# One lane for a group's loads, partial sums spread over the gate products, and layer 1's rows kept on chip in a two-layer graph network

## The chip, the cores and the metric

The kernel runs on one core of one Trainium2 chip. The metric is the device time of one execution in microseconds (us). The program writes its instructions engine by engine: TensorE (PE in the profile, with PEld for its weight loads) multiplies matrices, VectorE (DVE), ScalarE (ACT) and GpSimd (POOL) work on elements, and DMAs are issued from the queues of SyncE (SP), ScalarE and GpSimd. Each engine takes its instructions in the order in which they were written down, so an instruction that waits holds up all that stand behind it on the same engine.

## The reference, cut to what matters

There are 128 graphs of 128 nodes with 256 features, all in f32. Layer 0 normalizes the rows, runs two convolutions along the nodes and a sum over neighbours, and mixes the results with a gated unit. Layer 1 runs five small graph convolutions over the first 25 nodes of each graph.

```python
h = relu(layernorm(x))                       # layer 0
x_conv = relu(bn2(conv17(relu(bn1(conv1(h))))) + h)
A = exp(-dist(h @ w_se.T)) * adj
x_nmp = A @ relu(h @ w_msg.T + b_msg)        # sum over neighbours
gi = concat(x_conv, x_nmp) @ w_ih.T + b_ih
gh = h @ w_hh.T + b_hh
r, z = sigmoid(gi_r + gh_r), sigmoid(gi_z + gh_z)
n = tanh(gi_n + r * gh_n)
x = x + (1 - z) * n + z * h
h = relu(layernorm(x))                       # layer 1, nodes 0 to 24
for g, nodes in enumerate(GROUPS):           # two graph convolutions each
    fused[nodes] += softmax(fusion_w)[g] * gcn(gcn(h[nodes], W1[g]), W2[g])
x = x + fused
```

## The kernel before

Four graphs make a group; there are 32 groups (q = 0 to 31). Sixteen graphs, that is four groups, make a block of layer 1; there are eight blocks. The kernel is written as Python generators. A generator writes some instructions and then yields two numbers: how much TensorE time they are thought to take, and how long its next step should be left alone. Generators stand in lanes, lanes have weights, and a small planner (`Order.run`) always takes a step from the ready lane that has had least for its weight. The order in which the steps are taken is the order of the instructions on every engine. No time of the chip enters into it.

The work falls into these stages:

- **Setup** (`fold`, `load_taps`): x of the first groups, the constants, the 1x1 weights `c1w` and the 17-tap weights come in. `fold` normalizes the first group.
- **Stage a** (`stage_a`, 16 groups at a time): moments of the rows (L272 to L275), normalization (L280), transpose (L390), ReLU to `hT` (L392), the 1x1 convolution (L401, bias added by VectorE in L404) and a Fourier transform over the nodes (L412). `tap_weights` runs beside it: products of the taps (L455), copied by ScalarE (L460) and VectorE (L462), written to DRAM.
- **Stage b** (`stage_b`, L502): the 17-tap convolution as products in the Fourier domain, once for each half of the groups. `early` runs beside all of this and computes the sums over neighbours (L571 to L618) ahead, which go to DRAM.
- **Group stage**: for each group, `stage_n` loads `hT` and the neighbour sums `xm` and makes the four differences `tm` of `xm` on VectorE (`sums`, L551 to L554). `stage_c` transforms the convolution back (L663), forms the gate products (L698, seven for r and z with `wrz`, seven half ones with `wn`, on 256 columns each in a fast scheme that needs the differences `th`, `tm` and `tc` of its three operands), L762 for the hidden part, and adds the products up on VectorE (L730 to L793). Then come tanh (L795), the mixing on GpSimd (L798 to L801), a transpose back (L814) and the addition of x (L817 to L820). The first 32 rows of each graph, which layer 1 needs, go to DRAM (`x1d`, L826), the other rows to the output (L827). `th` of the next group is made in one go after the last hidden product. Two of the programs `stage_n`, `stage_c` are in work at a time, in one lane.
- **Layer 1**: `prepare` builds the normalized adjacency of a block, and `rows_of_x` in its course loads the block's rows from DRAM (L907), takes the moments of all four groups at once, raises to the power -1/2 on GpSimd (L275), normalizes (L280) and clips at zero on GpSimd (L901). `block` multiplies (L986, L1003, L1012), turns and gathers (L1033, L1045, L1054) and adds the result to the rows. This lane has weight 0.36 against 1 of the groups. The last block takes its rows from the chip (`direct`).

The gate products are held in three PSUM banks (`pgat`): TensorE can be three products ahead of VectorE, and then waits for a bank. All other products share five banks (`ptmp`).

Of the kernel before, what the change touches and what calls it, by code (L numbers as in the profile page):

```python
# [9 lines left out]
FP = mybir.dt.float32  # L10
# [197 lines left out]
def kernel(ctx: ExitStack, tc: tile.TileContext, x, adj, consts, vecs, w_se, conv1_w,  # L208
# [17 lines left out]
    x1d = [dr.tile([SB, WIDE, D], FP, name=f"x1d{b}") for b in range(NBLK)]  # L226
# [144 lines left out]
    def stage_a(q):  # L371
        ab = LATE["ab"]
        for n in range(q, min(q + 2, (q // BQ + 1) * BQ)):
            if n not in XA:
                load_xa(n)
                if n == q:
                    yield 0.0, 6.0
# [19 lines left out]
        for h in range(2):  # L397
# [9 lines left out]
            yield 1.75, 2.0 * h  # L407
# [31 lines left out]
    def tap_weights():  # L439

        yield 0.0, 0.0
        for n in range(4):
            if n:
                if n < 3:
                    load_taps(n + 1, nc.sync, nc.gpsimd)
                if n == 1:
                    load_late()
            for m in range(8):
# [87 lines left out]
    EN, IN, IN2, X1, E_DONE = {}, {}, {}, {}, set()  # L536
# [8 lines left out]
    TH, HT, TM = {}, {}, {}  # L545

    def sums(name, q, x, bufs=1):


        t = LATE["co"].tile([P, 4, D], FP, tag=name, name=f"{name}{q}", bufs=bufs)  # L550
        nc.vector.tensor_sub(t[:, 0], x[:, 0, D:], x[:, 0, :D])  # L551
        nc.vector.tensor_sub(t[:, 1], x[:, 1, D:], t[:, 0])  # L552
        nc.vector.tensor_sub(t[:, 2], x[:, 1, D:], x[:, 0, D:])
        nc.vector.tensor_sub(t[:, 3], t[:, 1], x[:, 1, :D])  # L554
        return t
# [81 lines left out]
    def stage_n(q):  # L637
        hT = LATE["co"].tile([P, 2, 512], FP, tag="hT", name=f"hTc{q}", bufs=2)
# [4 lines left out]
        HT[q] = hT  # L643
        TM[q] = sums("tm", q, xm, bufs=2)
        IN[q] = hT, xm

    def stage_c(q):
        while not (q - 1 in G_DONE and q in IN):
            yield 0.0, 0.5
        (hT, xm), tm = IN.pop(q), TM.pop(q)  # L650
# [6 lines left out]
        th = TH.pop(q) if q in TH else sums("th", q, hT)  # L657
# [77 lines left out]
        tcs = sums("tc", q, xc)  # L735
# [7 lines left out]
        sigmoid(r2, r2, 0)  # L743
        yield 2.6, 0.0
# [6 lines left out]
        sigmoid(z2, z2, 2)  # L751
        yield 2.6, 0.0
# [3 lines left out]
        sigmoid(z1, z1, 2)  # L756
        yield 2.6, 0.0

        for dc in range(2):
# [6 lines left out]
            if dc and q + 1 in HT:  # L766
                TH[q + 1] = sums("th", q + 1, HT.pop(q + 1))
# [40 lines left out]
        direct = X1.get(q // QS)  # L808
        for h in range(2):
# [6 lines left out]
            if h == 0 and direct is not None:  # L816
                nc.vector.tensor_add(direct[:, q % QS], xt[:, 0], po[:, 0])  # L817
                nc.vector.tensor_add(xt[:, 1], xt[:, 1], po[:, 1])
            else:
                nc.vector.tensor_add(xt[:, 2 * h:2 * h + 2], xt[:, 2 * h:2 * h + 2], po)  # L820
        yield 0.9, 1.5
        for j in range(GB):
            rows = xt[j * WIDE:(j + 1) * WIDE]
            g = q * GB + j
            if direct is None:
                nc.gpsimd.dma_start(out=x1d[g // SB][g % SB], in_=rows[:, 0])  # L826
            nc.gpsimd.dma_start(out=out[g, WIDE:].rearrange("(t n) c -> n t c", n=WIDE),  # L827
                                in_=rows[:, 1:4])
# [3 lines left out]
    S, B1_DONE, P_DONE, Y_DONE = {}, set(), set(), set()  # L832

    def setup_1():
# [39 lines left out]
        last = NBLK - 1  # L874
        X1[last] = S["pool2"].tile([P, QS, D], FP, tag="x1l", name=f"x1_{last}", bufs=1)
        P_DONE.add(-1)
        B1_DONE.add(-1)
        Y_DONE.add(-1)
# [8 lines left out]
    def rows_of_x(blk, wait=True):  # L887

        ready = all(q in C_DONE for q in range(blk * QS, (blk + 1) * QS))
        if blk in S or not (wait or ready and blk - 1 in Y_DONE):  # L890
            return
        while not (all(q in C_DONE for q in range(blk * QS, (blk + 1) * QS))
                   and blk - 1 in Y_DONE):
            yield 0.0, 0.5
        if blk not in X1:
            load_x1(blk)
            yield 0.0, 6.0
        pool2 = S["pool2"]
        x1h = S[blk] = pool2.tile([P, QS, D], FP, tag="x1h", name=f"x1h{blk}", bufs=1)
# [239 lines left out]
```

## Time and profile before

| what | us | from |
|---|---|---|
| device time, median of 3 runs (2208.85 to 2214.99) | 2210.95 | the times |
| span of the profiled run | 2210.7 | the page |
| TensorE busy | 2079.8 (94%) | the page, part 1 |
| VectorE busy | 1198.4 (54%) | the page, part 1 |
| GpSimd busy | 788.4 (36%) | the page, part 1 |
| ScalarE busy | 690.1 (31%) | the page, part 1 |
| mean granted clock of TensorE | 0.971 | the times |
| last matmul ends at | 2196.6 | the timeline |

TensorE is busy for nearly the whole span, and the chain that ended last lies on it for 83%. The share of the other engines is an average over stages. The page's slices are 55 us long, so that a pause of 5 us is a tenth of one slice and hardly shows; pauses have to be looked for in the table of stretches of 50 us and in the timeline. "Idle before" in a timeline is the time that the engine did nothing before the instruction, with the instruction that ended it.

### The profile page before, as it was taken

To read this page: it belongs to the slowest core of one execution; us is meant where nothing else is said; L and a number is where in the kernel's file an instruction comes from. 1 tells how busy PE (TensorE), PEld (TensorE's weight loads), DVE (VectorE), ACT (ScalarE), POOL (GpSimd) and SP (SyncE) were. 2 spreads that over 40 slices of the span, in tenths; PEclk is the share of its full clock that TensorE was granted. 3 is DMA by queue.
4 is the path that set the end of the run, shared out by engine and by line. 5 is a ranking of instruction groups with operands and counts; after the bars stand their busy time and mean duration, and the time that the engine had idled before them with its cause. 6 is when DMAs were issued, how large, how long until landed. Compare 5 with 4: busy or idle time off the path is not lost.

```text
span 2210.7 us, 30635 instructions
## 1 busy us (share of the span) xinstructions
PE 2079.8 (94%) x11124; PEld 1636.9 (74%) x11124; DVE 1198.4 (54%) x2659; ACT 690.1 (31%) x1511; POOL 788.4 (36%) x990
## 2 busy tenths in 40 slices
PE   4999999899999999999999999999999999999967
PEld 2667888788888777777767778677777777776855
DVE  3765444676444547654554564564564565465541
ACT  2654222344322333223322322322322322322322
POOL 2431466231465234333332342252242333333140
PEclk8999999999999999999999999999999999999988
DMA  9986777744777734323232333232332322332211
GB/s 163 267 244 195 237 262 259 215 144 134 238 261 253 229 92 121 84 71 89 76 103 79 91 90 88 65 94 84 86 91 69 94 75 80 101 85 71 77 34 39
DMA packets 194359, 288.97 MB, mean 131 GB/s; under 512 B 22877, under 2 KB 145762, under 8 KB 194210
## 3 DMA queue, kind: packets, MB, share of 16 engines
q1 hardware_dynamic: 159794, 188.48, 30.0%
q0 software_dynamic: 33584, 97.81, 14.0%
q8 instruction: 88, 1.44, 0.3%
q10 hardware_dynamic: 832, 0.74, 0.2%
q14 instruction: 61, 0.50, 0.1%
HBM read 191.01 MB, written 95.94 MB: 130 GB/s over the span
## 4 chain that ended last, share of the span: by engine, by line
PE 83%; DVE 7%; DMA 4%; issue 2%; POOL 2%; ACT 1%; SPq 1%; DVEq 0%; ACTq 0%; POOLq 0%
PE p L698 33%; PE pa L502 6%; PE pg L762 5%; PE ph L1003 5%; PE pz L1012 5%; PE pm L591 4%; PE pc L401 4%; PE pb L502 3%; PE pi L663 3%; PE px L616 2%; PE pf L412 2%; DMA xa<-in_x 2%; PE pg L1045 1%; PE pc L677 1%; DVE st L272 1%
## 5 line engine op out<-in xcount | busy, mean ns | idle before, releaser
L798 POOL TENSOR_TENSOR d<-hTc,r 128x512 f32<-128x512 f32 x64 | 84.3, 1317 | 508.4 <-ACT r L795 495.7
L502 PE MATMUL pa<-wf,X 128*128 128x256 f32 x640 | 154.2, 385 | 0.0
L698 PE MATMUL p<-tc,wrz 128*128 128x256 f32 x512 | 133.0, 382 | 1.5 <-DVE tc L552 1.0
L698 PE MATMUL p<-th,wrz 128*128 128x256 f32 x512 | 134.2, 385 | 0.0
L698 PE MATMUL p<-tm,wrz 128*128 128x256 f32 x512 | 133.2, 383 | 0.0
L502 PEld LDWEIGHTS pa<-wf,X 128*128 128x128 f32 x640 | 119.3, 192 | 17.5 <-issue 2.8
L275 POOL TENSOR_TENSOR rs<-rs,cst 128x4 f32<-128x4 f32 x40 | 42.0, 1049 | 250.7 <-DVE rs L274 243.6
L525 DVE SCALAR_TENSOR_TENSOR y<-pa,kk 128x512 f32<-128x512 f32 x78 | 53.8, 690 | 142.7 <-ACT kk L524 142.5
L401 PE MATMUL pc<-c1w,hTa 128*128 128x256 f32 x512 | 127.6, 399 | 0.3 <-ACT hTa L392 0.3
L591 PE MATMUL pm<-wmsg,hT 128*128 128x256 f32 x512 | 121.2, 381 | 0.0
L401 PEld LDWEIGHTS pc<-c1w,hTa 128*128 128x128 f32 x512 | 98.3, 199 | 29.2 <-issue 6.4
L711 ACT ACTIVATE r<-r,brz 128x256 f32<-128x256 f32 x128 | 58.0, 500 | 186.5 <-DVE r L742 157.3
L762 PE MATMUL pg<-hTc,whn 128*128 128x512 f32 x256 | 116.0, 593 | 0.0
L826 POOL DMA_DIRECT2D x1d<-xt x112 | 59.3, 530 | 150.5 <-DVE xt L820 147.2
L698 PEld LDWEIGHTS p<-tc,wrz 128*128 128x128 f32 x512 | 97.5, 192 | 17.9 <-DVE tc L552 4.7
L1003 PE MATMUL ph<-yz,w 128*128 128x96 f32 (+3 forms) x640 | 108.3, 322 | 0.5 <-DVE yz L988 0.5
L698 PEld LDWEIGHTS p<-tm,wrz 128*128 128x128 f32 x512 | 98.5, 192 | 13.7
L1012 PE MATMUL pz<-hh,w 128*128 128x96 f32 (+3 forms) x640 | 107.4, 321 | 0.0
L698 PEld LDWEIGHTS p<-th,wrz 128*128 128x128 f32 x512 | 94.8, 190 | 16.9 <-issue 4.9
L591 PEld LDWEIGHTS pm<-wmsg,hT 128*128 128x128 f32 x512 | 95.9, 190 | 15.3 <-issue 2.1
L698 PE MATMUL p<-tm,wn 128*128 128x256 f32 x256 | 80.6, 397 | 24.2 <-DVE v L777 24.2
L1003 PEld LDWEIGHTS ph<-yz,w 128*128 128x128 f32 x640 | 87.1, 190 | 21.8 <-issue 15.8
(198 smaller groups left out, 4587.4 us busy)
## 6 DMA issues: line engine op xcount, KB each, us to landing
wf<-wfd SPq DMA_DIRECT2D x160, 256.0 KB, 4.0
wfd<-ws POOLq DMA_DIRECT2D x64, 320.0 KB, 6.2
yd<-y POOLq DMA_DIRECT2D x80, 256.0 KB, 3.8
yt<-yd SPq DMA_DIRECT2D x64, 320.0 KB, 4.1
w<-in_W SPq DMA_DIRECT2D x40, 512.0 KB, 4.0
xa<-in_x SPq DMA_DIRECT2D x128, 128.0 KB, 4.7
hTd<-hTa POOLq DMA_DIRECT2D x32, 512.0 KB, 4.8
hT<-hTd SPq DMA_DIRECT2D x32, 512.0 KB, 6.5
```

What stands on the lines that cost most here:

```text
L401: nc.tensor.matmul(pc[:, i], hT[:, k, (2 * h + i) * N:(2 * h + i + 1) * N], c1w[:, k], start=(k == 0), stop=(k == 1))
L502: nc.tensor.matmul(ps, xk(k), WF[f][:, k, s], start=(k == 0), stop=(k == 1))
L525: nc.vector.scalar_tensor_tensor(y, pa, 2.0, kk[:, None].to_broadcast([P, 2, D]), op0=ALU.mult, op1=ALU.subtract)
L591: nc.tensor.matmul(pm[:, i], hT[:, k, j * N:(j + 1) * N], wmsg[:, k], start=(k == 0), stop=(k == 1))
L663: nc.tensor.matmul(pi[b * 64:(b + 1) * 64], inv[:F], yt[:, b::2], start=True, stop=True)
L698: nc.tensor.matmul(ps[:, m], w[:, i, k, m * P:(m + 1) * P], factor(i, x, t), start=first and j == 0, stop=last and j == len(n) - 1)
L711: nc.scalar.activation(dst[:, m], src[:, m], AF.Sigmoid, bias=brz[:, b + m:b + m + 1])
L762: nc.tensor.matmul(pg, whn[:, k, dc * P:(dc + 1) * P], hT[:, k], start=(k == 0), stop=(k == 1))
L798: nc.gpsimd.tensor_sub(d, hT[:, dc], r[:, dc])
L826: nc.gpsimd.dma_start(out=x1d[g // SB][g % SB], in_=rows[:, 0])
L1003: nc.tensor.matmul(ph, w1[:, k, m * P:(m + 1) * P], yz[:, k, :, o:o + n], start=(k == 0), stop=(k == 1))
L1012: nc.tensor.matmul(pz, w2[:, g, m, cc * P:(cc + 1) * P], hs[g][:, m], start=(m == 0), stop=(m == 3))
```

## The change

The change has four parts.

1. **Start and stage a.** `c1w` and x of the second group come ahead of the taps, x of the third is asked for before `fold`, the second set of taps comes only in the course of the first one's products, and the tap products begin 16 units later. In the second half, groups after the first wait 14 units for their load where it was 6, and one pause of stage a is 2.8 where it was 2.
2. **A lane for the loads.** `stage_n` only loads `hT` and `xm` now, in a lane of its own, as soon as the group two before has finished its gates; `hT` has three buffers.
3. **Sums in pieces.** The eight differences of `hT` and `xm` of the next group are written two, two, two, one and one at a time, after the r and z products and the hidden products (`some_sums`). `th` has two buffers.
4. **Layer 1's rows on chip.** The transpose back writes its first rows into a tile of the block, of which there are three. The DRAM tensor, its 112 writes and 28 reads are gone. A lane `rows` takes the moments, the power, the normalization and the ReLU one group at a time; the ReLU is on ScalarE now. Layer 1 may start on a group as soon as its own rows are there. Its weight is 0.2 instead of 0.36.

No matrix product is added or taken away.

```diff
@@ stage_a, tap_weights
-                    yield 0.0, 6.0
+                    yield 0.0, 14.0 if q > BQ else 6.0
...
-            yield 1.75, 2.0 * h
+            yield 1.75, 2.8 * h
...
-        yield 0.0, 0.0
+        yield 0.0, 16.0
@@ sums
+    def some_sums(q, n):
+        if q in IN:
+            if q not in SUMS:
+                hT, xm = IN[q]
+                (th, a), (tm, b) = sums("th", q, hT), sums("tm", q, xm)
+                SUMS[q] = th, tm, a + b
+            while SUMS[q][2] and n != 0:
+                SUMS[q][2].pop(0)()
+                n = n and n - 1
@@ stage_n
-        hT = LATE["co"].tile([P, 2, 512], FP, tag="hT", name=f"hTc{q}", bufs=2)
+        while q > 1 and q - 2 not in G_DONE:
+            yield 0.0, 0.5
+        hT = LATE["co"].tile([P, 2, 512], FP, tag="hT", name=f"hTc{q}", bufs=3)
...
-        TM[q] = sums("tm", q, xm, bufs=2)
@@ stage_c
+        some_sums(q + 1, 2)
...
-            if dc and q + 1 in HT:
-                TH[q + 1] = sums("th", q + 1, HT.pop(q + 1))
+            some_sums(q + 1, 1)
...
+            X1[blk] = fr.tile([P, QS, D], FP, tag="x1", name=f"x1_{blk}", bufs=3)
...
-            if direct is None:
-                nc.gpsimd.dma_start(out=x1d[g // SB][g % SB], in_=rows[:, 0])
@@ rows, in place of rows_of_x
+        nc.vector.bn_stats(st, x1)
+        nc.vector.bn_aggr(mv, st)
+        nc.vector.tensor_scalar(rs, mv[:, 1:2], EPS, None, op0=ALU.add)
+        nc.gpsimd.tensor_tensor(rs, rs, c("mhalf")[:, :1], ALU.pow)
+        yield 0.0, 2.5
+        x1h = S["x1h", q] = S["pool"].tile([P, D], FP, tag="x1h", name=f"x1h{q}", bufs=5)
+        nc.vector.tensor_scalar(x1h, x1, mv[:, 0:1], rs, op0=ALU.subtract, op1=ALU.mult)
+        nc.scalar.activation(x1h, x1h, AF.Relu)
@@ start and lanes
-    load_taps(0, nc.sync, nc.gpsimd, nc.scalar)
     nc.scalar.dma_start(out=c1w, in_=conv1_w.rearrange("(k p) o -> p k o", p=P))
     load_xa(1)
+    load_taps(0, nc.sync, nc.gpsimd, nc.scalar)
+    load_xa(2)
     fold()
-    load_taps(1, nc.sync, nc.gpsimd)
...
-    groups = Lane([stage(q) for q in range(NQ) for stage in (stage_n, stage_c)], ahead=2)
+    loads = Lane([stage_n(q) for q in range(NQ)])
+    groups = Lane([stage_c(q) for q in range(NQ)], ahead=2)
...
-    order.run(groups, beside, Lane(second, ahead=2, weight=0.36))
+    order.run(loads, groups, beside, Lane([rows(q) for q in range(NQ)], ahead=2),
+              Lane(second, ahead=2, weight=0.2))
```

## The prediction

> **What bounds the kernel now.** First the page's parts 1 and 2: TensorE is busy 94% of the span, so only its pauses (2210.7 - 2079.8 = 131 us) and its slow clock can be gained; no product is removed. The clock row falls at both ends.
>
> ```profile
> PE 2079.8 (94%) x11124; PEld 1636.9 (74%) x11124; DVE 1198.4 (54%) x2659; ACT 690.1 (31%) x1511; POOL 788.4 (36%) x990
> ...
> PEclk8999999999999999999999999999999999999988
> ```
>
> Next I went through TensorE's timeline for pauses over 0.5 us. Apart from the first 15.6 us, in which nothing has arrived, four places hold most: 15.1 us from 23 to 38, 8.3 us from 406 to 414, seven pauses of 4.6 to 4.9 us between 936 and 1995, about 175 us apart (one for each layer-1 block but the last), and 16.7 us in three pieces from 2136 to 2155. The rest is about 30 us around stage a and 14 us for the last output after the last matmul.
>
> The start, from the timeline. DVE stands in front of the second group's x at 22.2 and of the third's at 35.2. Behind that wait is the copy of the tap products at 37.5, and TensorE, out of banks, waits for this copy.
>
> ```profile
> 35.18 0.43 DVE L272 BATCH_NORM_STATS2 st<-xa 128x6 f32<-128x256 f32 x1 [10.51 <-DMA xa<-in_x]
> 37.44 0.17 DVE L274 TENSOR_SCALAR rs<-mv 128x4 f32<-128x4 f32 x1
> 37.52 1.28 DVE L462 COPY ws<-pw 80x512 f32<-80x512 f32 x2
> ...
> 38.25 1.99 PE L455 MATMUL pw<-wt,cst 17*80 17x512 f32 x4 [15.12 <-DVE ws L462]
> ```
>
> The second half's start. TensorE has done its neighbour work at 405.7 and waits for the first normalized rows; DVE takes the moments of three groups (403.9 to 411) before it normalizes the first at 413.5.
>
> ```profile
> 413.49 3.96 DVE L280 TENSOR_SCALAR xa<-xa,mv,rs 128x256 f32<-128x256 f32 x12
> 414.00 3.96 PE L390 MATMUL ph<-cst,xa 128*128 128x128 f32 x16 [8.33 <-issue]
> ```
>
> The group stage. TensorE's waits from 900 to 2100 have two lines of weight, both for a VectorE addition that frees a gate bank. The timeline of one shows why: between 933.5 and 940.6 DVE does the moments of four groups, waits 1.2 us for GpSimd's power, normalizes four times and makes four differences, all ahead of the addition.
>
> ```profile
> PE p L698 <- DVE v L777: 24.2, 5, 4.8
> PE p L698 <- DVE v L783: 9.2, 2, 4.6
> ```
>
> ```profile
> 933.50 0.42 DVE L272 BATCH_NORM_STATS2 st<-x 128x6 f32<-128x256 f32 x1
> ...
> 937.08 1.38 DVE L280 TENSOR_SCALAR x1h<-x,mv,rs 128x256 f32<-128x256 f32 x4 [1.16 <-POOL rs L275]
> ...
> 940.56 0.41 DVE L777 TENSOR_TENSOR v<-v,p 128x256 f32<-128x256 f32 x1
> ...
> 941.02 1.22 PE L698 MATMUL p<-tm,wn 128*128 128x256 f32 x2 [4.84 <-DVE v L777]
> 942.04 1.06 PE L698 MATMUL p<-tc,wn 128*128 128x256 f32 x2
> ```
>
> After such a pause the pairs start 0.85 to 1.02 us apart, where 0.43 is usual: the clock is halved for some time. Summing the excess, I find 1.5 us after the pause at 936 and 2.9 us after that at 1111.
>
> The end. After the last gate product (2136.2) nothing is left for TensorE but what hangs on the last group: mixing on GpSimd, transposes, moments of four groups, power, normalization, clipping, then L986.
>
> ```profile
> 2144.75 1.76 PE L814 MATMUL po<-cst,z 128*128 128x128 f32 x7 [3.42 <-POOL z L801]
> ...
> 2155.14 5.01 PE L986 MATMUL py<-r,x1h 128*128 128x212 f32 x16 [8.64 <-POOL x1h L901]
> ...
> 2160.63 7.65 PE L1003 MATMUL ph<-yz,w 128*128 128x400 f32 x32 [0.47 <-DVE yz L988]
> ```
>
> **What the Trainium skill says.** "TensorE: Matmul & The Clock Gate", section "What's actually happening", has two clock states, full and half; an idle window of about 3.4 us leads to the half one, and about 3.4 us of work out of it. The trace agrees: after 4.8 us of idling the pairs take twice 0.43 us, for 3 to 5 us. So a pause costs more than its length, and one shortened below that size may cost nothing extra. "DMA: Bandwidth & Descriptors", section "Issuing engines are not separate DMA queues", says that transfers asked for by SP, ACT and POOL run on the same 16 engines and interleave: moving the taps behind x gives x their bandwidth. Here the DMA share is 0.91 in the first 50 us at 150 GB/s, which fits. "SBUF — State Buffer", section "Who interferes with whom", says that a VectorE operation with two SBUF inputs contends with a GpSimd one that reads SBUF. The trace agrees: the differences at 945.6 to 949.4, beside GpSimd's mixing, took 1.02 to 1.49 us, others 0.42. Moved behind the r and z products they meet it less.
>
> **The change part by part.** Where an order is named, it is the order in which the changed program's instructions stand on each engine.
>
> *Start.* In the new order VectorE takes the moments of groups 0, 1 and 2 ahead of the first bias addition, and TensorE has the whole 1x1 convolution of group 0 in front of the wait. So it still waits for the third x. Bytes ahead of this: 3 x 0.5 MB of x, 1.1 MB of taps, 0.45 MB of constants and c1w, about 3.1 MB; before it was 4.25 MB at 35 us, 0.12 MB a us, so 26 us. With 2.4 us of moments the wait ends near 29 instead of 38: -9 us. Bounds: -4 (the smaller start only delays later loads; the DMAs stay 0.91 busy to 150 us) and -13 (x lands sooner).
>
> *Second half.* Moments of one group instead of three stand before the first normalization: 2 x 2.4 us less, and these, where the load has landed, now lie beside the two message products. TensorE has as much neighbour work before the wait as before. I take 8.3 to about 2 us, and the half clock after it (16 transposes took 3.96 us, some 2 us too much) goes: -8 us, bounds -4 and -10.
>
> *Rows and sums.* A group's row work on VectorE is now 0.42 + 0.18 + 0.17 us, then 0.35 us (a quarter of 1.38). In the new order the normalization stands behind the addition for z1 and two differences, so that GpSimd's power (1.04 us) has 1.5 us or more and a product's time to finish; ahead of it on GpSimd are only four output DMAs (0.55 us each). From the addition for r2 to the last hidden product VectorE has 0.69 + 4 x 0.69 + 8 x 0.42 + 1.1 + 2 x 0.75, some 9.4 us, in three products of 2.6 us and one of 3.4, 11.2 us, plus what layer 1 puts between. Nothing stands in front of L777 now but one difference. All seven pauses should go: 33.4 us, and 7 x 2.2 us of half clock (mean of the two measured), 15 us: -48 us. If half of that stays, -24.
>
> *Loads.* `hT` and `xm` are asked for a group ahead; landing takes 5.0 and 4.7 us in the DMA table, and the first difference comes some 13 us of products later. Behind `xm` on SP's queue stand `yt` and x; `xm` waits for the last product of two groups earlier, which has just been issued. Nothing on the path, 0 us.
>
> *DRAM.* 112 writes (GpSimd busy 59.3 us) and 28 reads go, 22 us of clipping moves from GpSimd to ScalarE (32 x about 0.4 us), and GpSimd gets 24 more powers, 25 us. In the group stage GpSimd is busy 119 of 350 us, ScalarE 102, the DMAs 0.31. These engines are hidden: 0 us.
>
> *End.* In the new order block 6 is wholly behind the last gate product, with block 7 after it. That moves TensorE work, it doesn't add any. Block 6 fills the 16.7 us, and the half clock there (L986 5.0 us for 2.9, L1003 7.65 for 5.5) goes, 4 us: -21 us. A second block without groups beside it has the small waits of the last one's end (0.3 to 1 us each, some 3 us in all): -18 us. Bounds -12 and -21.
>
> Sum: 9 + 8 + 48 + 18 = 83 us. I leave 3 us for small new pauses in places that changed order: -80, 2211 - 80 = **2131 us**.
>
> **The rivals.** *VectorE's queue still blocks.* The work is only cut up, and VectorE's total is hardly less; if the pieces fall between the short `wn` products (0.87 us each), half the pauses stay: 2131 + 24 = 2155. For it: 0.87 us is about two VectorE operations. Against: six of eight differences and the moments lie before these.
> *Layer 1 lags.* Its weight falls from 0.36 to 0.2, two blocks run alone at the end, and if these stall on their chains the end gains nothing and loses 4: 2131 + 22 = 2153. For it: the new order's end. Against: block 7 alone took 41.5 us with under 3 us of pauses once warm.
> *The power moves onto the path (slower).* GpSimd's six mixing operations (1.3 us each, 7.7 us) could stand ahead of a group's power, with VectorE's queue waiting behind. Three banks cover 2.6 us; 3 us for each of 32 groups in TensorE's path are 96 us: 2131 + 96 = 2227. For it: L280 waits 1.2 us for the power in every block. Against: in the new order the power precedes the mixing.
> *More.* Stage a's other pauses and their half clock go too: 2108.
>
> **How the numbers follow.** The forecast has 0.68, VectorE 0.14, the lag 0.08, the slower case 0.03, more 0.07. Within the forecast the four bounds give 2131 - 15 and + 25. The range takes in the rivals up to 2155 and most of the lower bounds: 2106 to 2160. Faster 0.96, same 0.01, slower 0.03.
>
> **What would show it.** Right: no wait of TensorE over 2 us between 900 and 2100 and a clock of 1.00 there; TensorE's first long pause ends near 29; under 3 us before the 17th group's transposes; no pause over 2 us between the last gate product and the last block. Wrong: waits of L280 or its successor for the power; TensorE waiting for VectorE in the `wn` products; waits for `hT`, `xm` or `yt`; or a DMA share that makes stage a end as late as before.

## The result, and the profile after

The changed kernel takes 2147.28 us, the median of four runs (2143.28 to 2148.42); the kernel before, run beside it, took 2209.96 us (four runs). The ratio is 0.9709, with a 95% interval from 0.9689 to 0.9729: faster by 62.7 us or 2.9%. The forecast was 2131 us with a range of 2106 to 2160. The direction and the range held; the forecast was 16 us too hopeful, and the experiments show that this 16 is the sum of larger errors of both signs.

The lines are shifted a little in the new kernel: the gate products are L706 (before L698), the sums L551, layer 1's first product L989 (L986), its large one L1006 (L1003), the mixing L810 to L813 (L798 to L801), the row moments, power, normalization and ReLU of a group L904 to L911.

The page of the kernel after, parts 1 and 2:

```profile
PE 2070.0 (97%) x11124; PEld 1631.5 (76%) x11124; DVE 1153.1 (54%) x2711; ACT 703.6 (33%) x1545; POOL 720.6 (34%) x894
...
PEclk9999999999999999999999999999999999999999
```

TensorE is 9.8 us less busy with the same 11124 products (the clock), and it is idle for 2141.4 - 2070.0 = 71.4 us of the profiled span where it was 130.9. So most of the gain is pauses, a smaller part is clock. The table has the pauses between the same pieces of work in both traces: the length of the stretch less TensorE's busy time in it. The ends of matmuls are modelled, so the entries are approximate.

| stretch | idle before, us | idle after, us |
|---|---|---|
| start to the first product of stage b (at 237.1 before, 208.4 after) | 44.5 | 30.3 |
| stage b and stage a of the second half (to 745.2, 711.5) | 14.8 | 10.8 |
| transition to the group stage (to 930, 892) | 4.4 | 11.8 |
| rest of the group stage, to the last gate product (2136.2, 2041.9) | 34.1 | 3.4 |
| last gate product to the last matmul (2196.6, 2134.6) | 19.0 | 8.4 |
| last matmul to the end of the span | 14.0 | 6.8 |

The start in TensorE's timeline: the long wait ends at 25.9 where it ended at 38.2, but the wait for the copies of the tap products at 80, which was 1.7 us, is 3.6 now. ScalarE, which makes these copies, stands for 5.5 us until earlier tap products (`wfd`) are written to DRAM.

```profile
25.88 2.25 PE L389 MATMUL ph<-cst,xa 128*128 128x128 f32 x8 [3.35 <-issue]
...
81.46 1.08 ACT L458 ACTIVATE ws<-pw 80x512 f32<-80x512 f32 x2 [5.48 <-DMA wfd<-ws]
...
82.10 1.58 PE L453 MATMUL pw<-wt,cst 17*80 17x512 f32 x8 [3.57 <-ACT ws L458]
```

The group stage. First TensorE's waits between 900 and 2040 us (in total, times, longest), then the stretch from 1060 to 2040 (its length, then busy us and instructions of PE, PEld, DVE, ACT and POOL, the granted clock, the DMA share, GB/s). Of the seven waits for an addition of the `wn` products nothing is left: 978.9 busy us of 980, where the kernel before had 950.9. The clock is 0.99 and not 1.00: some stretches of half clock remain there, though no pause of 1 us is left.

```profile
PE p L706 <- ACT u L737: 1.9, 1, 1.9
PE py L989 <- ACT x1h L911: 1.5, 3, 0.8
```

```profile
1060.00:2040.00 980.00, 978.87 (x4791) 756.30 (x4790) 528.08 (x1225) 302.92 (x642) 283.00 (x326) 0.99 0.28 80
```

The transition, in the timeline of all engines. Three waits of 3.1 to 3.7 us are new, and each has the same shape: one or two pieces of work for the next stage stand on VectorE ahead of what TensorE needs.

```profile
721.06 0.42 DVE L551 TENSOR_TENSOR th<-hTc 128x256 f32<-128x256 f32 x1
...
725.94 1.44 PE L624 MATMUL px<-aT,msg 128*128 128x128 f32 x5 [3.15 <-DVE aT L616]
...
829.41 1.28 ACT L872 ACT_TABLE_LOAD   x1
...
830.95 0.16 DVE L874 TENSOR_REDUCE fsm<-fus 128x1 f32<-128x5 f32 x1 [2.72 <-ACT fus L872]
...
834.17 1.79 PE L706 MATMUL p<-tc,wrz 128*128 128x256 f32 x4 [3.68 <-DVE tc L551]
...
880.36 0.77 DVE L932 TENSOR_REDUCE dg<-b 25x16 f32<-25x400 f32 x2 [1.62 <-POOL b L927]
...
884.81 0.98 PE L989 MATMUL py<-r,x1h 128*128 128x212 f32 x4 [3.15 <-ACT x1h L911]
```

At 721 these are the eight sums of the first group, in one go between two additions of the neighbour messages. At 831 VectorE waits 2.72 us for an Exp on five numbers, which ScalarE can't start before it has loaded a table. At 880 VectorE waits for GpSimd's adjacency in front of a normalization. After each of them the clock is low too: 0.90 between 700 and 750 us, 0.95 between 800 and 850, 0.92 between 850 and 900.

The end, all engines:

```profile
2042.34 1.27 POOL L810 TENSOR_TENSOR d<-hTc,r 128x512 f32<-128x512 f32 x1 [18.56 <-ACT r L807]
...
2050.16 1.08 POOL L907 TENSOR_TENSOR rs<-rs,cst 128x1 f32<-128x1 f32 x2
2050.76 0.41 DVE L910 TENSOR_SCALAR x1h<-x,mv,rs 128x256 f32<-128x256 f32 x1 [5.64 <-POOL rs L907]
2051.09 0.37 DVE L991 COPY yz<-py 128x212 f32<-128x212 f32 x1
...
2051.51 1.70 PE L1006 MATMUL ph<-yz,w 128*128 128x400 f32 x2 [6.10 <-DVE yz L991]
```

The power of two groups stands on GpSimd behind the six mixing operations of the last group. VectorE's normalization waits 5.64 us for it, the copy of block 6's `py` stands behind that, and TensorE waits 6.10 us for the copy, after which 16 products take 8.11 us on a slow clock.

### The profile page after: what moved, and what is told of

Its sections match the earlier page's. It is cut to its first block, busy times and chain, and to the rows that moved or that the text cites. A ratio compares the mean times of both kernels' runs of the same rounds, so it can differ in the third digit from the quotient of the medians.

```text
span 2141.4 us, 30439 instructions
## 1 busy us (share of the span) xinstructions
PE 2070.0 (97%) x11124; PEld 1631.5 (76%) x11124; DVE 1153.1 (54%) x2711; ACT 703.6 (33%) x1545; POOL 720.6 (34%) x894
## 4 chain that ended last, share of the span: by engine, by line
PE 87%; DVE 4%; DMA 3%; POOL 2%; issue 1%; ACT 1%; SPq 0%; ACTq 0%; POOLq 0%; DVEq 0%
PE p L706 35%; PE pa L500 7%; PE pg L775 5%; PE ph L1006 5%; PE pz L1015 5%; PE pm L599 5%; PE pc L400 3%; PE pb L500 3%; PE px L624 3%; PE pi L671 3%; PE pf L411 2%; DMA wfd<-ws 2%; PE pg L1049 1%; PE po L830 1%; PE pc L685 1%
## 5 line engine op out<-in xcount | busy, mean ns | idle before, releaser
L810 POOL TENSOR_TENSOR d<-hTc,r 128x512 f32<-128x512 f32 x64 | 81.6, 1276 | 389.2 <-ACT r L807 389.2
L839 POOL DMA_DIRECT2D out<-xt x128 | 72.1, 569 | 249.9 <-DVE xt L836 245.6
L706 PE MATMUL p<-tc,wrz 128*128 128x256 f32 x512 | 132.3, 381 | 4.1 <-DVE tc L551 4.1
L706 PE MATMUL p<-th,wrz 128*128 128x256 f32 x512 | 132.6, 382 | 1.9 <-ACT u L737 1.9
L706 PE MATMUL p<-tm,wrz 128*128 128x256 f32 x512 | 132.3, 381 | 0.0
L400 PE MATMUL pc<-c1w,hTa 128*128 128x256 f32 x512 | 122.0, 384 | 3.5 <-ACT ef L587 2.2
L775 PE MATMUL pg<-hTc,whn 128*128 128x512 f32 x256 | 120.9, 615 | 0.0
L1006 PE MATMUL ph<-yz,w 128*128 128x96 f32 (+3 forms) x640 | 114.4, 335 | 6.6 <-DVE yz L991 6.6
L1006 PEld LDWEIGHTS ph<-yz,w 128*128 128x128 f32 x640 | 92.0, 201 | 29.2 <-issue 15.7
L1008 ACT ACTIVATE hh<-ph,vec 128x96 f32<-128x96 f32 (+3 forms) x160 | 64.2, 403 | 147.3 <-PE ph L1006 138.1
L688 DVE SCALAR_TENSOR_TENSOR xc<-pc,s_bn,hTc 128x256 f32<-128x256 f32 x128 | 53.1, 477 | 110.4 <-PE pc L685 110.4
L706 PEld LDWEIGHTS p<-tc,wrz 128*128 128x128 f32 x512 | 97.6, 191 | 18.2 <-DVE tc L551 4.9
L706 PEld LDWEIGHTS p<-tm,wrz 128*128 128x128 f32 x512 | 97.9, 191 | 13.5
L706 PEld LDWEIGHTS p<-th,wrz 128*128 128x128 f32 x512 | 95.6, 191 | 14.1 <-ACT u L737 2.3
```

The costliest lines, as they stand in the source:

```text
L400: nc.tensor.matmul(pc[:, i], hT[:, k, (2 * h + i) * N:(2 * h + i + 1) * N], c1w[:, k], start=(k == 0), stop=(k == 1))
L706: nc.tensor.matmul(ps[:, m], w[:, i, k, m * P:(m + 1) * P], factor(i, x, t), start=first and j == 0, stop=last and j == len(n) - 1)
L775: nc.tensor.matmul(pg, whn[:, k, dc * P:(dc + 1) * P], hT[:, k], start=(k == 0), stop=(k == 1))
L810: nc.gpsimd.tensor_sub(d, hT[:, dc], r[:, dc])
L839: nc.gpsimd.dma_start(out=out[q * GB + j, WIDE:].rearrange("(t n) c -> n t c", n=WIDE), in_=xt[j * WIDE:(j + 1) * WIDE, 1:4])
L1006: nc.tensor.matmul(ph, w1[:, k, m * P:(m + 1) * P], yz[:, k, :, o:o + n], start=(k == 0), stop=(k == 1))
```

## The experiments

The theory: the seven pauses were made by the *place* of layer 1's row work on VectorE's queue, ahead of additions that free gate banks of the short `wn` products. That the rows stay on chip, that row work is done by single groups and that the sums are spread are then side matters. The rival: these things themselves are what pays. All ratios are against the kernel before on the same chip; each kernel had four runs.

**The start alone.** The kernel before with part 1 of the change.

```diff
-    load_taps(0, nc.sync, nc.gpsimd, nc.scalar)
     nc.scalar.dma_start(out=c1w, ...)
     load_xa(1)
+    load_taps(0, nc.sync, nc.gpsimd, nc.scalar)
+    load_xa(2)
     fold()
-    load_taps(1, nc.sync, nc.gpsimd)
... (and the three other pauses of part 1)
```

> The kernel before with part 1 of the change alone (order of the first loads, tap products later, pauses of stage a). Theory (the prediction's own sum): the start gives 9 us and the second half 8, so 2210 - 17 = 2193 us, the first long pause of TensorE ends near 26 us, as in the changed kernel, and the pause of 8.3 us at 406 is gone. Rival (stage a is bound by the DMAs, whose share is 0.91 to 1.00 up to 150 us, so that an earlier start is given back as waits for the tap writes): the second half alone remains, 2202 us or more. The seven pauses of the group stage and the 16.7 us at the end must stand as before in either case.

Measured: 2199.39 us, ratio 0.9939 (0.9922 to 0.9955), 13.5 us less than the kernel before beside it. The first wait ends at 26.6 and the 8.3 us at the 17th group are gone. Two waits grew: that at 80 from 1.7 to 4.3 us (again the copies stand until tap products are written, which is the rival in part) and one at 188 from 2.9 to 3.7. The seven pauses and the 16.7 us at the end stand as they were. The gain is 10 to 17 us by the interval, so that the forecast's 17 lies at its edge.

One of the three waits of the transition is here already, with nothing of parts 2 to 4: the Exp has come to stand ahead of the sums for `tc`.

```profile
829.66 0.16 DVE L861 TENSOR_REDUCE fsm<-fus 128x1 f32<-128x5 f32 x1 [2.72 <-ACT fus L859]
...
833.01 1.13 PE L697 MATMUL p<-tc,wrz 128*128 128x256 f32 x4 [3.78 <-DVE tc L551]
```

So it is part 1, by shifting where the setup of layer 1 falls, that brings this wait, and its cost is inside the 13.5 us.

**The sums in bursts.** The change, with `tm` made at the load and `th` in one go after the last hidden product, as before.

```diff
-        some_sums(q + 1, 2)          # three times
-            some_sums(q + 1, 1)
+            if dc:
+                some_sums(q + 1, None)
@@ stage_n
+        (th, a), (tm, b) = sums("th", q, hT), sums("tm", q, xm)
+        for operation in b:
+            operation()
+        SUMS[q] = th, tm, a
```

> The changed kernel with the sums in bursts again: four differences of xm as soon as it is loaded, four of hT after the last hidden product. Theory (the seven pauses came from a burst of row work and differences together, 7 us of VectorE in front of one addition): four differences are 1.7 us, which the three banks cover (2.6 us), so no wait of TensorE over 1 us between 1060 and 2040, and 2147 us within 4. Rival (the differences alone are enough to run the banks dry in the short products): a wait of 1 us or more in most of the 32 groups, 2170 us or more.

Measured: 2143.88 us, ratio 0.9693 (0.9671 to 0.9714), not told apart from the change's 0.9709, and again no pause between 1060 and 2040 us. Spreading the sums isn't needed for the gain, once the row work is elsewhere. It does do two things that the total doesn't show: the wait for `tc` in the transition is 7.2 us here against 3.7, and VectorE is busy 43.5 us longer (1196.6 against 1153.1) with the same 2711 instructions. Made at the load, the second difference of `xm` meets GpSimd's mixing and takes 1.37 us in the median, where the change has 0.43.

**Row work by blocks.** The change, with moments, power, normalization and ReLU of four groups together, still on chip.

```diff
-    def rows(q):
-        while not (q in C_DONE and -1 in P_DONE and (q < 5 or q - 5 in PY_DONE)):
+    def rows(blk):
+        while not (all(q in C_DONE for q in qs) and -1 in P_DONE
+                   and (blk < 2 or all(q - 2 * QS in PY_DONE for q in qs))):
...
+        mv, rs = moments(X1[blk], "b")
+        yield 0.0, 2.5
+        for q in qs:      # normalize, eight x1h buffers; then the ReLU of all four
```

> The changed kernel with layer 1's row work for four groups at once (moments, one power, four normalizations, four ReLUs), still on chip, with eight row buffers. Theory (the burst in front of an addition is what makes a pause, wherever the planner puts it): 4 x 0.6 us of moments and 1.4 us of normalizations in each block now stand among the additions of the r and z products, of which three banks hold 7.8 us, so short pauses at most, 2147 to 2155 us. If the size of the burst alone counts: seven pauses of 3 us with half clock after them, 2147 + 7 x 5 = 2182 us.

Measured: 2126.6 us, ratio 0.9608 (0.9589 to 0.9628): not slower than the change but 21 us faster. The row work of four groups is together again, 2.4 us of moments and 1.4 us of normalizations with two additions and two differences between them. In the written order it stands among the r and z products (between the additions L752 and L767), which last 2.6 us each, and the only pauses of over 1 us at it are two of 1.5, where layer 1's first product waits for the rows. So it isn't the splitting by groups either. The pauses at 881 and at the end are gone as well. The run has eight tiles for the normalized rows where the change has five, and the next run shows that these alone are worth 12 of the 21 us; some 9 are left for the blocks.

**More buffers for the normalized rows.** The change with eight `x1h` tiles in place of five.

```diff
-        while not (q in C_DONE and -1 in P_DONE and (q < 5 or q - 5 in PY_DONE)):
+        while not (q in C_DONE and -1 in P_DONE and (q < 8 or q - 8 in PY_DONE)):
```

> The changed kernel with eight buffers for the normalized rows where it has five, so that groups 29 and 30 need not wait for block 6 to use its rows, and their power stands in front of the last group's mixing on GpSimd. Theory (the 6.1 us that TensorE waits at 2045 come from VectorE's copies standing behind two normalizations that wait for a power behind 7.7 us of mixing): the pause goes, and the half clock after it in part, 2147 - 6 to - 12 = 2135 to 2141 us. Rival (the end is bound by the last group's own chain, mixing to transposes): the pause moves to the transposes, 2147 us within 3.

Measured: 2135.31 us, ratio 0.9650 (0.9632 to 0.9668), 12 us faster than the change. The pause of 6.1 us at the end and the slow products behind it are gone: with five tiles the last rows had to wait for block 6's `py`, and so their power was written behind the mixing of the last group. The three pauses of the transition stand unchanged (3.14, 3.65 and 3.15 us).

**The burst moved in the kernel before.** The most direct run: nothing of the change but another place for the burst.

```diff
@@ rows_of_x, in the kernel before
+        while not RZ and len(G_DONE) < NQ:
+            yield 0.0, 0.5
         pool2 = S["pool2"]
@@ stage_c: RZ is set after the sigmoid of r2 and cleared after that of z1
```

> The kernel before with one edit: layer 1's burst of row work (moments of four groups, power, four normalizations, clipping) waits in the planner until the r and z products of a group are being written, so that it stands between the additions for z2 and z1 in place of ahead of a wn addition. Rows still go through DRAM, the differences stay in one go, nothing else changes. Theory (place alone makes the seven pauses): the seven pauses of 4.6 to 4.9 us and their half clock go, -33 - 15 = -48 us, 2213 - 48 = 2165; with pauses of 1 to 2 us left for the four differences of the neighbour sums ahead of the first wn addition, up to 2175. Rival (the rows have to be on chip, or the sums in pieces): 2205 to 2213.

Measured: 2164.6 us against 2211.39, ratio 0.9809 (0.9767 to 0.9852): 46.8 us from moving one burst, with the trip through DRAM, the clipping on GpSimd and the sums in one go all as before. One of the four runs took 2179.65, the others 2163.66 to 2164.93, so the interval is wide, 33 to 52 us, and whether the gain exceeds 2% is not settled. The burst is still one piece of 4.9 us, now between additions of z products. Its first instruction on VectorE, and the addition right behind it:

```profile
960.91 0.42 DVE L272 BATCH_NORM_STATS2 st<-x 128x6 f32<-128x256 f32 x1
...
965.79 0.68 DVE L757 TENSOR_TENSOR z<-u,p 128x512 f32<-128x512 f32 x1
```

TensorE's waits from 900 to 2040, and the stretch to the last gate products (columns as above):

```profile
PE p L699 <- DVE z L757: 5.7, 6, 1.0
```

```profile
900.00:2085.00 1185.00, 1177.49 (x5864) 908.09 (x5863) 662.52 (x1437) 352.53 (x755) 407.86 (x495) 1.00 0.31 86
```

The seven pauses of 4.6 to 4.9 us have become six of at most 1.0 us (one more, of 1.1, is at a hidden product), and the clock is 1.00. On the page TensorE's busy time falls from 2079.8 to 2059.9 us and its idle time from 130.9 to 102.6: 28 us of pauses and 20 us of half clock. Of the pauses 26 lie at the seven places and 2 at the end. So half clock came to 2.5 to 2.8 us for each of the seven, an estimate, as a little of the 20 belongs to the end.

**The burst late, rows on chip.** The kernel with row work by blocks, its burst held back by 8 units and written in one go.

```diff
+        yield 0.0, 8.0
         mv, rs = moments(X1[blk], "b")
-        yield 0.0, 2.5
```

> The kernel of e3_rows_block with its burst moved: moments of four groups, power and four normalizations stand in one go 8 units later, ahead of an addition that frees a bank of the short wn products (L789 or L793), in place of among the r and z products. Rows stay on chip and the sums stay in pieces. Theory (it is the place on VectorE's queue that makes the seven pauses, not the size of the burst, the DRAM trip or the one-go sums): 2.4 us of moments, 0.2, some 1.2 us wait for the power and 1.4 us of normalization are 5.2 us against about 2.6 us that three banks cover, so pauses of about 2.5 to 3.5 us come back in each of seven blocks, some with a little half clock: 2127 + 7 x 3 = 2148, with half clock up to 2160. Rival (pauses went because rows come from the chip, whatever the place): no pause, 2127, within 3 us of e3_rows_block.

Measured: 2147.78 us, ratio 0.9709 (0.9686 to 0.9733), 21 us more than with the burst early, as large as the theory said. That is luck, since the pauses weren't where it said. The edit also makes one piece of what stood in two, so that place and wholeness change together here. Three of 3.7 to 3.9 us are waits of layer 1's own first product for the rows, which now stood right in front of it; one of 3.6 us is a wait for ScalarE, whose ReLU stood there too; only one, of 1.3 us, is at a `wn` product. The timeline of one:

```profile
924.10 2.13 PE L988 MATMUL py<-r,x1h 128*128 128x212 f32 x5 [3.87 <-ACT x1h L910]
```

**The same with the sums in bursts.** Both bursts together, as the order was before.

```diff
@@ on the kernel with sums in bursts and row work by blocks
+        yield 0.0, 8.0
         mv, rs = moments(X1[blk], "b")
-        yield 0.0, 2.5
```

> e5_rows_late with the sums in bursts too: the four differences of the neighbour sums at their load, the four of h in one go after the last hidden product, so that moments, power, normalizations and four differences stand next to each other as in the kernel before, but with the rows on chip. Theory (length of VectorE's work ahead of a wn addition against three banks): 1.5 us more in each block, so pauses of 4 to 5 us as in the kernel before and their half clock: 2127 + 7 x 4.8 + 7 x 2.2 = 2176, at least 12 us more than e5_rows_late. Rival (sums don't matter, as in e2_sums_burst): same as e5_rows_late within 4 us.

Measured: 2159.72 us, ratio 0.9761 (0.9740 to 0.9781), 12 us more than with the late burst alone, at the lower edge of the theory's figure. But the mechanism under test has the smaller part of it. Two waits for `x1h` grow from 3.9 to 5.0 us, where four differences stand in the same run of work, and one for ScalarE from 3.6 to 4.1: 2.7 us in all. The wait for `tc` at 830, which has no late burst in front of it, grows by more, from 2.9 to 6.7, much as it did with the bursts of sums alone, and most of the rest is clock. That spread sums help a burst that stands badly is seen in these 2.7 us and no more.

**Writes to DRAM back.** The kernel with row work by blocks, and the rows written to DRAM again, unread.

```diff
+            nc.gpsimd.dma_start(out=x1d[q // QS][q % QS * GB + j],
+                                in_=X1[blk][j * WIDE:(j + 1) * WIDE, q % QS])
```

> e3_rows_block with the 128 writes of rows to a DRAM tensor put back on GpSimd's queue (nothing reads them; 0.53 us of issue each, 68 us in all). Theory (the trip through DRAM was hidden): 0 us, within 3 us of e3_rows_block, 2124 to 2130. Rival (GpSimd's queue holds up the power or the mixing, hence VectorE): four issues of 0.53 us stand ahead of the power of a block or of layer 1's GpSimd work: 2 us for each block and at the end, 2127 + 16 = 2143. If the span again ends 14 us after the last matmul, the writes to DRAM are what the 7 us at the end belong to.

Measured: 2129.67 us, ratio 0.9623 (0.9605 to 0.9641); the interval overlaps that without the writes. GpSimd is busy 65 us longer (772.7 to 707.5), and hardly any of it is seen.

**The transition put in order.** The kernel with row work by blocks and four edits of the planner's pauses.

```diff
@@ stage_c, first group only
+        while q == 0 and (q not in SUMS or SUMS[q][2]):
+            some_sums(q, 2)
+            yield 0.0, 1.5
@@ setup_1
+        yield 0.0, 3.0
         nc.scalar.activation(fus, fus, AF.Exp)
+        yield 0.0, 6.0
@@ prepare, between GpSimd's additions and VectorE's sums over them
+        yield 0.0, 9.0
...
-        yield 0.0, 7.0
+        yield 0.0, 2.0
@@ rows
-        yield 0.0, 1.5
+        yield 0.0, 4.0
```

> e3_rows_block with four edits of the planner's order around 720 to 1100 us: the first group's eight sums in four pieces between the last neighbour work; setup_1 gives way before and after its Exp so that VectorE's softmax of five numbers doesn't stand waiting ahead of the tc sums; prepare gives way 9 units between GpSimd's additions and VectorE's sums over them; layer 1 starts 4 units after the ReLU in place of 1.5. Theory (these waits are queue order, not missing work): pauses of 3.1, 2.9, 1.5, 1.9 and 1.5 us go, and with them the half clock of 0.85 to 0.95 in 700 to 850 us: 11 + 8 = 19 us less at most, 2127 - 12 = 2115, range 2107 to 2120. Rival (the pauses move to the next instruction in line): 2123 to 2130.

Measured: 2115.26 us, ratio 0.9556 (0.9537 to 0.9574): 4.4% faster than the kernel before and the fastest of all. The stretch from 700 to 900 us has a clock of 1.00 and 198.1 busy us of 200:

```profile
700.00:900.00 200.00, 198.07 (x1072) 158.00 (x1073) 118.64 (x280) 68.60 (x144) 63.42 (x80) 1.00 0.43 126
```

Against the change with eight buffers, which has the end mended but not the transition, TensorE's busy time is 12.6 us less (2065.9 to 2053.3) and its idle time 7.6 us less (65.0 to 57.4). That is 20 us, but the runs differ in the row work by blocks as well. Between 700 and 900 us the kernel with eight buffers has 11.7 us of pauses and a clock of 0.97, this one 1.9 us and 1.00. So the transition held some 10 us of pauses and up to 6 of clock, about 16 us.

**The late burst without a product behind it.** The last kernel with the burst late again, but layer 1 starting 8 units after it, so that only gate banks can make TensorE wait.

```diff
+        yield 0.0, 8.0
         mv, rs = moments(X1[blk], "b")
-        yield 0.0, 2.5
...
-        yield 0.0, 4.0
+        yield 0.0, 8.0
```

> e8_transition with the burst late again as in e5_rows_late (moments, power and normalization in one go ahead of L780, L792 or L796, the wn additions), but layer 1 starts 8 units after the ReLU, so that no product of layer 1 stands right behind the burst. It shows the wait for a gate bank by itself. Theory: 5.2 us on VectorE against about 2.6 us that three banks cover: a pause of some 2.5 us in each of seven blocks, at the gate products of wn, no long half clock: 2115 + 18 = 2133. Rival (in e5 only layer 1's products behind the burst waited, the banks cover it): 2115 to 2120.

Measured: 2141.1 us, ratio 0.9682 (0.9665 to 0.9700), 26 us more than without the delay. The pauses stand at gate products now: 1.9 and 1.8 us in the first block, 4.25 in the second, 4.0 in the third, 1.7 in the seventh, and two of 1.5 to 2.1 us at layer 1's products in between. One in the timeline:

```profile
1089.18 0.42 DVE L271 BATCH_NORM_STATS2 st<-x 128x6 f32<-128x256 f32 x1
...
1092.76 1.38 DVE L912 TENSOR_SCALAR x1h<-x,mv,rs 128x256 f32<-128x256 f32 x4 [1.15 <-POOL rs L274]
...
1094.49 0.37 ACT L790 ACTIVATE v<-p 128x256 f32<-128x256 f32 x1
...
1094.91 1.22 PE L709 MATMUL p<-tm,wn 128*128 128x256 f32 x2 [4.25 <-ACT v L790]
```

The theory's bank wait is there, and larger than its 2.5 us. In the pause shown, the ReLU of the four groups stood on ScalarE ahead of the copy L790, and VectorE waited 0.75 us for this copy. But the pause of 4.0 us in the third block is ended by a VectorE addition, with no wait for ScalarE. What was too large in both is the cover: TensorE stopped 1.5 us after the burst began in the block shown (1089.2 to 1090.7) and 1.7 us after it in the third, and not 2.6, presumably because products already held some of the banks. About half of the 26 us is clock: TensorE's busy time is 13.0 us longer than without the delay.

**Layer 1's weight back.** The kernel with the transition in order, and weight 0.36 for layer 1.

```diff
-              Lane(second, ahead=2, weight=0.2))
+              Lane(second, ahead=2, weight=0.36))
```

> e8_transition with layer 1's weight at 0.36 again, as in the kernel before. Block 6 is then done before the last gate product, and only block 7 is left for the end. Theory (block 6 fills the wait for the last group's mixing, transposes and rows): the 16.7 us of pauses in three pieces and about 4 us of half clock come back: 2115 + 18 = 2133. Rival (with row work by the quicker chain on chip the end is short anyway): 2115 to 2120.

Measured: 2126.48 us, ratio 0.9614 (0.9597 to 0.9631), 11 us more, between the two expectations. The three pauses of the kernel before are back after the last gate product, the third shorter (5.25 us where it was 8.64; the kernel before had one clip of all four rows on GpSimd, 2.8 us, in that chain):

```profile
2068.96 0.33 PE L833 MATMUL po<-cst,z 128*128 128x128 f32 x1 [4.68 <-POOL z L816]
...
2072.86 1.75 PE L833 MATMUL po<-cst,z 128*128 128x128 f32 x7 [3.57 <-POOL z L816]
...
2079.86 2.49 PE L994 MATMUL py<-r,x1h 128*128 128x212 f32 x6 [5.25 <-ACT x1h L915]
```

**The whole trip through DRAM back.** The kernel with the transition in order; rows written, read again, and moments and normalization taken of what was read.

```diff
+        xr = S["pool"].tile([P, QS, D], FP, tag="xr", name=f"xr{blk}", bufs=1)
+        for j in range(GB):
+            nc.sync.dma_start(out=xr[j * WIDE:(j + 1) * WIDE], in_=x1d[blk]...)
+        yield 0.0, 6.0
-        mv, rs = moments(X1[blk], "b")
+        mv, rs = moments(xr, "b")
```

> e8_transition with the whole trip of the rows through DRAM put back: 128 writes on GpSimd's queue, four reads for each block on SyncE's and the planner's 6 units of waiting for them, and moments and normalization of what was read. With these 6 units the burst slips to the hidden and wn products in the written order. Theory (transfers hidden, but the slip puts the burst ahead of wn additions): 2 us in each of seven blocks, 2115 + 14 = 2129, pauses at L781, L793 or L797. Rival (transfers late as well): VectorE's moments wait for the read rows, 2140 and more; other rival: 2115 to 2119, nothing to be seen. If the span again ends 14 us after the last matmul, the reads are what the 7 us at the end belong to; if 7 us, neither writes nor reads are.

Measured: 2115.63 us, ratio 0.9566 (0.9551 to 0.9581): no difference from the kernel without the trip. The theory's 14 us were wrong. The burst did slip behind the hidden products, but cut in two, moments in one place and normalization in another, and its pauses in the group stage are two of 1.5 us and one of 1.1. Together with the late burst of the run before last, which was one piece, it suggests that a late burst hurts when it is written in one go.

## Why the prediction was right, and where it was off

**The seven pauses: right, with the right size.** The forecast was -48 us (33.4 of pauses, 15 of clock). Moving the burst alone in the kernel before gave -46.8, some 28 of pauses and 20 of clock. The move left waits of up to 1 us behind, and half clock was put a little low at 2.2 us a pause. The account of the mechanism in the prediction was the place on VectorE's queue, and that is what the runs confirm. What the change says it does there is not what pays: neither the spread sums, nor the split by groups, nor the saved trip through DRAM is needed, each put back alone within the interval or, for the split, faster. What the change did was to move the burst. A part of that comes from the planner's order alone: with row work by blocks in the lane `rows`, nothing but that order puts it among the r and z products. One term is too generous: three banks were taken to cover 2.6 us, and with a late burst they covered 1.5 to 1.7.

**The start and the second half: right within the interval, by errors that cancel.** Forecast -17, measured -13.5 for part 1 alone (10 to 17). The wait at the start ended even earlier than forecast (25.9, not 29), and the pause of 8.3 us went wholly. The sum for the start took 0.12 MB a us and 3.1 MB; in the traces the DMAs had moved 4.9 MB by 35.2 us before (0.14 MB a us) and 4.2 MB by 26 us after (0.16), so more bytes came faster. Set against it are losses that the terms for part 1 left out: the longer wait at 80, where copies stand until tap products are written; four pauses of 1.3 to 2.2 us in stage a of the second half, 7.1 us in sum, where there were 9.6, so that most of the 8.3 us came back in pieces; and the wait of 3.8 us for `tc` at 833.

**"+3 for small new pauses in places that changed order": the step that failed most.** The transition alone has 7.4 us more of pauses than before and a lower clock (0.94 where it was 1.00), and mending it gave about 16 us. The prediction followed the order of the steady group stage and of the end, but not of the 150 us in which the group stage begins. There the first group's eight sums have no r and z products to hide behind, the setup's Exp waits for a table of 1.28 us with VectorE standing behind it (the Trainium skill, "ScalarE activation tables: per-element evaluation and per-set limits", section "What a function is on this engine", has the same figure, 1283 ns, for a switch between two sets), and the block's first rows wait behind the adjacency. The places of all three can be seen in the written order. In the kernel before the Exp stands among `wn` products and VectorE waits 0.27 us for it.

**The end: the mechanism right, half kept.** Block 6 does fill the old wait for the last group (with weight 0.36 three pauses of 13.5 us in all come back, +11 us). But the rival in which the power stands behind GpSimd's mixing came true in this one place, with the prediction's own sign of being wrong, a normalization that waits for the power (5.64 us): a pause of 6.1 us and a slow clock, 12 us in all by the run with eight buffers. The prediction argued it away for all groups because the power precedes the mixing in the steady order; at the end five buffers turn that order round.

**Not foreseen: 7 us behind the last matmul**, where the span ends 6.8 us after it, not 14.0. So a part of the gain came without a reason in the prediction, which is luck.

The two runs on the kernel before add up to 13.5 + 46.8 = 60.3 of the 62.7 us. The other pieces nearly cancel: in the table of pauses the end and the time after the last matmul gain 10.6 and 7.2 us, the transition loses 7.4, and half clock in the transition takes more. That the total came within 16 us of the forecast is in part this cancelling. One sum of the forecast is wrong: its four bounds allow 4 + 2 + 0 + 3 = 9 us on the lower side, not 15, and 5 + 4 + 24 + 6 = 39 on the upper one, or 25 only if they are taken as independent.

**Hidden work: right as far as it was tested.** The trip through DRAM costs nothing: writes 0, writes and reads 0 within the intervals. No run puts the old order of the loads (part 2) or the clipping on GpSimd back alone, so that these cost nothing, or help, is not shown. Spreading the sums did take them out of GpSimd's way, as the prediction said, and VectorE's 43.5 us were worth nothing in the total. The other rivals fell: VectorE's queue doesn't block in the new order (it does when the burst is put late, 21 to 26 us), and the lag of layer 1 is a gain.

## What to carry to other kernels

When an engine works through one queue, ask where a burst stands before asking how long it is: 5 us of row work in one piece cost 1 us of waiting behind products of 2.6 us and about 7 us a time more, with the slow clock, between products of 0.87 us. A change of order must be followed through the transitions too, where the work that hides things in the steady state isn't there yet or is no longer there. A change that does four things is best taken apart: here one effect, the place of a burst, is worth about three quarters of the gain, and one part, the split by groups, cost some 9 us.

## What the runs showed of the hardware that was not expected

The length of a pause did not decide by itself whether the clock went to half. With row work by blocks a pause of 2.94 us is followed by four products at full speed (1.13 us), and a moment later four take 1.92 us, where 1.03 is usual. In the same trace half clock sets in right after a pause of 1.93 us. With eight buffers a pause of 3.15 us has full clock behind it. First the kernel with row work by blocks, then the one with eight buffers:

```profile
835.60 1.13 PE L706 MATMUL p<-tc,wrz 128*128 128x256 f32 x4 [2.94 <-DVE tc L551]
...
837.94 1.92 PE L706 MATMUL p<-th,wrz 128*128 128x256 f32 x4
...
1044.58 1.59 PE L706 MATMUL p<-tc,wrz 128*128 128x256 f32 x4 [1.93 <-DVE tc L551]
```

```profile
883.97 0.98 PE L989 MATMUL py<-r,x1h 128*128 128x212 f32 x4 [3.15 <-ACT x1h L911]
884.79 1.03 PE L706 MATMUL p<-th,wrz 128*128 128x256 f32 x4
```

What the traces do have in common is a grid. In the kernel with row work by blocks the recorded clock goes to half at 727.7, 836.9 and 1045.1 us, 32 and 61 steps of 3.413 us apart, and stays there for three steps the first time and for one step after that; all its stretches of half clock but the one cut off by the end of the span are whole numbers of this step. The Trainium skill, "TensorE: Matmul & The Clock Gate", section "What's actually happening", puts the idle window at about 3.4 us; the step agrees with that, but half clock after 1.93 us of idling doesn't fit a whole window of it. Where a pause falls on the grid may be what counts; no run varied that.

The time from the last matmul to the end of the span is 14.0 us in the kernel before and in the two kernels that keep its layer 1 (the start alone, the burst moved), and 6.8 to 6.9 us in all others. The four last output transfers are the same in both, issued in 2.2 to 2.3 us, and in the kernel before the DMAs are idle from 2201.6 on, 9 us before the end. What differs is DRAIN, an instruction of GpSimd in the closing part of the program, the longest of its three: 11.09 us in the kernel before, 3.89 us after (the third number, in ns).

```profile
L1135 POOLq DRAIN  x3: 46/102/11085, 2198.8 to 2210.4; - x3
```

```profile
L1142 POOLq DRAIN  x3: 46/102/3891, 2136.8 to 2141.2; - x3
```

The kernel with writes, and that with writes and reads of the rows, both end after 6.8 us, so that it isn't the trip through DRAM. It is 11.1 us in the two kernels named as well, and 3.9 to 4.0 us in all others. The three kernels with the long DRAIN are those in which GpSimd clips the rows of layer 1; no run put that clipping back alone, so the cause stays open.
